# Identity and ones matmuls for three sums of a sparse-plus-polynomial attention layer (four-layer GNN, fp32)

## The chip, the cores and the metric

The kernel runs on one core of a Trainium2 chip. The metric is the device time of one execution in microseconds; three runs of the kernel before gave 3329.15, 3336.72 and 3339.13 us, and the median, 3336.72 us, is "the time before". Lower is better.

## The reference

Four graph layers over N = 2708 nodes with 128 features, all fp32, each on the ReLU of a layer norm of x and added back to x. Only layer 1 is touched by the change. With n nodes, H = 8 components and a reshape that mixes nodes and columns, it computes

```
q = (x @ Wq.T).reshape(d, n, h)          # d = 128 heads, h = 8
k = (x @ Wk.T).reshape(d, n, h)
v = (x @ Wv.T).reshape(d, n, h)
a = einsum('dnh,dmh->dnm', q, k) * d ** (-0.5)
a = softmax(a + adj + adj, axis=2)
out = einsum('dnm,dmh->dnh', a, v).reshape(n, h * d)
x = x + out @ Wo.T
```

So there are 128 heads (the index d), and each has queries, keys and values of only 8 components. adj is sparse: about four random entries in a row and the diagonal.

## The kernel before, in words

Layer 1 is not computed as 128 dense 2708 x 2708 attentions. The logits q.k are small, so exp(q.k) is written as a polynomial of degree 4. The sum over all nodes m then factors into products of monomials, and only the few neighbours of a node, where adj is not zero, are handled exactly by an added term with the weight exp(2 adj) - 1.

**The polynomial, one head at a time** (`for d in range(D)` in the block under `tc.manual_schedule()`, 128 heads; the order of every instruction there is the order in which the Python code issues it). N is cut into NT = 22 row tiles of 128 (the last has 20 rows), and these into NCH = 6 chunks of 4, 4, 3, 4, 4, 3 tiles; `parts` are the two halves of 11 tiles.
- `keys(d)` and `queries(d)` build, from the eight components, B_ALL = 9 second monomials (one and the eight components, in bk and bq) and F_ALL = 128 first monomials (fk and fq). ScalarE makes copies and squares (L717 to L719), `features` makes the products: for queries all by VectorE (L1147), for keys by GpSimd (L1150) except one of the last four products, which VectorE makes. `copies` (L1163) puts keys and queries in PSUM for VectorE.
- `with_values(d, h)` makes y, the values (8 and a one, VW = 9) times the second monomials of the key (copy by ScalarE L1181, product by GpSimd L1150).
- `moments(d, ...)` sums fk times y over the nodes on TensorE into m_ps (L1200), `weighted(d)` scales the result into mw (VectorE, L1210).
- `turn(d, c)` transposes the query monomials of a chunk on TensorE into f_ps (L1226), ScalarE copies them to fT (L1228). f_ps lies in the pool ps_t, which has a single PSUM buffer under the tag "tr".
- `evaluate(d, c)` multiplies fT by mw on TensorE into g_ps (L1238). VectorE multiplies by the query's second monomials into z (L1246), and **adds over the nine second monomials** with a reduction into o_raw (L1252).
- In a chunk the order is evaluate(d, c), turn(d, c+1), moments(d+1, ...), so a head's moments are made a head ahead; the sixth chunk has no moments.
- `prepare(g)` loads a group of GRP = 4 heads into raw and also **adds up all values** of the four heads: VectorE reduces raw over the row tiles (v_part, L806), TensorE adds over the partitions with ones (v_t, L813 and L815), VectorE copies to v_sum (L817). `sums(g)`, after the last head of a group, adds v_sum (the constant term of the polynomial) to o_raw on GpSimd (L824) and stores o_g.

**Beside it** a generator `first` is stepped 1.5 times in every chunk (PACE): `by_node` rewrites keys, values and queries by node to DRAM (n_kv, n_q, ScalarE L855, two groups to a store), `sorted_rows` loads the sorted lists of neighbours, and `from_neighbours` takes 121 blocks. A block is one neighbour slot for 128 nodes: a gather c_kv (GpSimd DMA, L915), the products of key and query for 128 heads times 8 components c_z (GpSimd, L930), **their sum over the eight components** c_c (VectorE reduction, L936), exp and weight (ScalarE, L943 and L944), weight times value c_v (VectorE, L954), and the accumulation over a node's slots on TensorE with an identity into v_ps (L971). After a tile's last slot `store` copies v_ps to c_acc (L986) and the result is scattered to more_n.

When `first` has ended, `step` runs `normalise` (load o_g and more_n, GpSimd adds them L1047, VectorE divides L1051 and L1052, store) and `project_out` (load o_cr, eight matmuls with woT, L676). woT, the transposed Wo, is made ahead of the loop by `load_wo` (L659 to L666).

Bold names the three sums that the change moves.

Of the kernel before, what the change touches and what calls it, by code (L numbers as in the profile page):

```python
# [45 lines left out]
def gnn4_kernel(  # L46
# [610 lines left out]
    def load_wo(lp, wk_pool, ps, tag):  # L657
        wo_nat = wk_pool.tile([P, HD], FP, name="wo_nat", tag=tag)
        nc.sync.dma_start(wo_nat, wo)  # L659
        wo_h = wo_nat.rearrange("p (c k) -> p k c", k=HEAD)  # L660
        woT = lp.tile([P, HEAD, C], FP, name="woT")
        for k0, kw in _cuts(HEAD, 4):
            pt = ps.tile([P, 4, C], FP, name="wo_ps", tag="tr")
            for k in range(kw):
                nc.tensor.transpose(pt[:, k], wo_h[:, k0 + k], ident)
            nc.vector.tensor_copy(woT[:, k0 : k0 + kw], pt[:, :kw])  # L666
        return woT
# [18 lines left out]
    with ExitStack() as ph:  # L686
# [3 lines left out]
        tm = ph.enter_context(tc.tile_pool(name="l1_tm", bufs=2))  # L690
        sm = ph.enter_context(tc.tile_pool(name="l1_sm", bufs=2))
        fp = ph.enter_context(tc.tile_pool(name="l1_f", bufs=2))
        ftp = ph.enter_context(tc.tile_pool(name="l1_ft", bufs=3))
# [11 lines left out]
        def features(mul, k, b, f, kp=None, other=None):  # L705


            n, T = k.shape[:2]
            kp = k if kp is None else kp
            kh = kp.rearrange("p t (h e) -> p t h e", h=2)  # L710
            ks = k.rearrange("p t (h e) -> p t h e", h=2)
            two, two_s = (a.rearrange("p t (x w) -> p t x w", w=2) for a in (kp, k))
            inn = b[:, :, 9:21].rearrange("p t (h e) -> p t h e", h=2)
            crs = b[:, :, 21:29].rearrange("p t (h e) -> p t h e", h=2)
            mul2, kp2 = (mul, kp) if other is None else other
            kh2 = kp2.rearrange("p t (h e) -> p t h e", h=2)
            nc.scalar.copy(b[:, :, 1:9], k)  # L717
            nc.scalar.copy(f[:, :, :8], k)
            nc.scalar.activation(inn[:, :, :, :4], ks, AF.Square)  # L719
            mul(  # L720
                inn[:, :, :, 4:6],
                two[:, :, :, 0].rearrange("p t (h x) -> p t h x", h=2),
                two_s[:, :, :, 1].rearrange("p t (h x) -> p t h x", h=2),
            )
            yield
            for a in range(2):
                mul(
                    crs[:, :, :, 2 * a : 2 * a + 2],
                    kh[:, :, :, 2:4],
                    ks[:, :, :, a : a + 1].to_broadcast([n, T, 2, 2]),  # L730
                )
                yield
            o = 8
            for h in range(2):
                mul(
                    f[:, :, o : o + 16].rearrange("p t (a b) -> p t a b", a=4),
                    kh[:, :, h, :, None].to_broadcast([n, T, 4, 4]),
                    inn[:, :, h, None, :4].to_broadcast([n, T, 4, 4]),
                )
                yield  # L740
                o += 16
            three = f[:, :, o : o + 8].rearrange("p t (h a b) -> p t h a b", h=2, a=2)
            for a in range(2):
                mul(
                    three[:, :, :, a],
                    kh[:, :, :, 2 - 2 * a : 4 - 2 * a],
                    inn[:, :, :, 4 + a : 5 + a].to_broadcast([n, T, 2, 2]),
                )
                yield
            o += 8  # L750
            for src, w in ((inn, 6), (crs, 4)):
                for h in range(2):
                    m, of = (mul2, kh2) if w == 6 and h else (mul, kh)
                    m(
                        f[:, :, o : o + 4 * w].rearrange("p t (a b) -> p t a b", a=w),
                        src[:, :, h, :, None].to_broadcast([n, T, w, 4]),
                        of[:, :, 1 - h, None, :].to_broadcast([n, T, w, 4]),
                    )
                    yield
                    o += 4 * w  # L760
            assert o == F_ALL
# [25 lines left out]
        def prepare(g, got):  # L787
# [6 lines left out]
            for e, at in enumerate((q_at, k_at)):  # L794
# [9 lines left out]
            v = raw[:, :, :, 2 * HEAD :]  # L804
            part = sm.tile([P, GRP, VW], FP, name="v_part")
            nc.vector.reduce_sum(  # L806
                part, v[:, :, :NF].rearrange("p i t k -> p i k t"), axis=AX.X
            )
            yield
            pt = ps_t.tile([P, BK], FP, name="v_t", tag="tr")  # L810
            to = pt[:, : GRP * VW]
            flat = part.rearrange("p i k -> p (i k)")
            nc.tensor.matmul(to, ones, flat, start=True, stop=not REM)  # L813
            if REM:
                nc.tensor.matmul(to, ones[:REM], v[:REM, :, NF], start=False, stop=True)  # L815
            vs = sm.tile([P, GRP, VW], FP, name="v_sum")
            nc.vector.tensor_copy(vs.rearrange("p i k -> p (i k)"), pt[:, : GRP * VW])  # L817
            got.append((raw, vs))
            yield

        def sums(g, ro):

            vs = got[g][1]
            nc.gpsimd.tensor_tensor(  # L824
                ro, ro, vs[:, None].to_broadcast([P, NT, GRP, VW]), ALU.add
            )
            nc.sync.dma_start(o_g[g], ro.rearrange("p t i k -> p (t i k)"))

        def by_node():
# [11 lines left out]
            for j in range(NG):  # L841
# [3 lines left out]
                if j % 2 == 0:  # L845
                    kv = lp.tile(
                        [P, NT, 2, GRP, 2, HEAD], FP, name="n_kv", tag="n_kv", bufs=2
                    )
                    qn = lp.tile([P, NT, 2, GRP, HEAD], FP, name="n_q", bufs=1)
# [8 lines left out]
                if j % 2:  # L858
                    hs = slice((j - 1) * GRP, (j + 1) * GRP)
# [31 lines left out]
        def from_neighbours():  # L891
# [34 lines left out]
            def logits(b):  # L926
                t, s0, w = todo[b]
                sz = rows[t][1]
                zs[b] = tm.tile([P, C, HEAD], FP, name="c_z", tag="tmp")
                nc.gpsimd.tensor_tensor(zs[b][:sz], kvs[b][:sz, 0, :, 0], qs[t][:sz], ALU.mult)  # L930

            def summed(b):
                t, s0, w = todo[b]
                sz = rows[t][1]
                cs[b] = c_two[:, b % 2, 0]
                nc.vector.reduce_sum(cs[b][:sz], zs.pop(b)[:sz], axis=AX.X)  # L936

            def weigh(b):
# [3 lines left out]
                c = cs[b][:sz]  # L942
                nc.scalar.activation(c, c, AF.Exp)  # L943
# [5 lines left out]
            def values(b):  # L949
# [3 lines left out]
                vs[b] = z = tm.tile([P, 2, BK // HEAD, HEAD], FP, name="c_v", tag="c_v")  # L953
# [10 lines left out]
            def added(b):  # L964
# [3 lines left out]
                if s0 == 0:  # L968
                    accs[t] = ps_v.tile([P, 2, BK], FP, name="v_ps")
                for j in range(2):  # L970
# [4 lines left out]
                        start=s0 == 0,  # L975
# [5 lines left out]
            def store():  # L981
                while done:
# [7 lines left out]
                    nc.scalar.copy(acc[:sz, :, HEAD], dens.pop(t)[:sz])  # L990
# [8 lines left out]
            if REM:  # L999
                none = tm.tile([P, C // 2 * VW], FP, name="none", tag="tmp")  # L1000
                nc.gpsimd.memset(none, 0.0)
# [7 lines left out]
            for b in range(M + 2):  # L1009
                if b + 1 < M:  # L1010
                    load(b + 1)
                yield
# [4 lines left out]
                if 0 < b <= M:  # L1017
                    weigh(b - 1)
                if 1 < b:
                    added(b - 2)  # L1020
                yield
# [3 lines left out]
                yield  # L1025
                if b < M:
                    summed(b)
# [5 lines left out]
        def normalise(g, ring):  # L1033

            if ring == "tm":
                ro = tm.tile([P, NT, GRP, VW], FP, name="r_raw", tag="tmp")
# [25 lines left out]
        woT = load_wo(lp, big, ps_t, "big")  # L1062
# [20 lines left out]
        def bank(t):  # L1083

            if not banks:
                banks.append(ps_v.tile([P, 2, BK], FP, name="v_ps"))
            return banks[0][:, t % 2, :C]

        def begin(summed):

            if not beside or beside[0][1] >= summed:
# [4 lines left out]
            for ring in ("tm", "big") if norm else ("big",):  # L1096
                if len(rings[ring]) < room[ring]:
                    beside.pop(0)
                    gen = (
                        normalise(i, ring) if norm else project_out(big, "big", bank, woT, i)  # L1100
# [57 lines left out]
        def copies(dk, dq):  # L1158

            kq = ps_q.tile([P, 2, NT, HEAD], FP, name="kq_ps")  # L1160
            for i, (what, d, at) in enumerate((("k", dk, k_at), ("q", dq, q_at))):
                if d is not None and d < D:
                    nc.scalar.copy(kq[:, i], got[d // GRP][0][:, d % GRP, :, at])  # L1163
                    copied[what, d] = kq[:, i]

        def keys(d):

            k = got[d // GRP][0][:, d % GRP, :, k_at]
# [3 lines left out]
        def with_values(d, h):  # L1172
# [3 lines left out]
            v = got[d // GRP][0][:, d % GRP, t0:t1, 2 * HEAD :]  # L1176
# [11 lines left out]
        def queries(d):  # L1188

            k = got[d // GRP][0][:, d % GRP, :, q_at]  # L1190
# [3 lines left out]
        def moments(d, h, n0, n1):  # L1194

            if d not in pms:
                pms[d] = ps_m.tile([P, BK], FP, name="m_ps")
# [32 lines left out]
        def evaluate(d, c):  # L1230
            h, t0, n = chunks[c]
            g, i = d // GRP, d % GRP
            if g not in ros:
                ros[g] = kp.tile([P, NT, GRP, VW], FP, name="o_raw")
            pg = ps_g.tile([P, 4, BK // 4], FP, name="g_ps")
            ft = fts.pop((d, c))
            for m in range(n):
# [7 lines left out]
            z = tm.tile([P, 4, VW, B_ALL], FP, name="z")  # L1245
            nc.vector.tensor_tensor(  # L1246
                z[:, :n],
# [4 lines left out]
            nc.vector.reduce_sum(  # L1252
                ros[g][:, t0 : t0 + n, i],
                z[:, :n],
                axis=AX.X,
            )

        with tc.manual_schedule():
# [20 lines left out]
            for d in range(D):  # L1279
                asked = queries(d + 1) if d + 1 < D else iter(())  # L1280
                for c in range(NCH):
# [16 lines left out]
                    elif d + 1 < D:  # L1298
                        turn(d + 1, 0)
                    if d + 1 < D and c < len(at):  # L1300
# [16 lines left out]
                g = d // GRP  # L1317
                if d % GRP == GRP - 1:
                    sums(g, ros.pop(g))
# [4 lines left out]

            nc.vector.memset(top, 0.0)
# [447 lines left out]
```

## Time and profile before

| | us |
|---|---|
| median of the three runs | 3336.72 |
| the profiled execution, its own time | 3354.19 |
| the span of that execution on the core | 3352.4 |
| busy PE (matmul) / PEld (weight load) | 2691.7 / 2273.0 |
| busy DVE / POOL / ACT | 2202.7 / 2009.3 / 1314.8 |

The profiled execution is 17.5 us longer than the median. The loop over heads runs from 563 us (its first mw) to 2830 us of the span; the text calls 563 to 970 us stage A (by_node beside the heads, 24 heads), 970 to 2373 us stage B (the neighbours' blocks, 81 heads) and 2373 to 2830 us stage C (normalise and project, 23 heads). What comes before is layer 0 and the making of q, k and v; what comes after is layers 2 and 3.

In the profile's lines, PE is TensorE's matmul, PEld its weight load, DVE is VectorE, ACT is ScalarE, POOL is GpSimd, SP the queue that issues most DMAs. Every fp32 matmul that is not a transpose stands in the trace as two records ("passes" in the text), each with a weight load of its own: L1238 issues 2816 matmuls and has 5632 records. A matmul's record lasts past the start of the next one, since they are pipelined; what a pass occupies is the distance from its start to the next start.

### The profile page before, as it was taken

To read this page: it belongs to the slowest core of one execution; us is meant where nothing else is said; L and a number is where in the kernel's file an instruction comes from. 1 tells how busy PE (TensorE), PEld (TensorE's weight loads), DVE (VectorE), ACT (ScalarE), POOL (GpSimd) and SP (SyncE) were. 2 spreads that over 40 slices of the span, in tenths; PEclk is the share of its full clock that TensorE was granted. 3 is DMA by queue.
4 is the path that set the end of the run, shared out by engine and by line. 5 is a ranking of instruction groups with operands and counts; after the bars stand their busy time and mean duration, and the time that the engine had idled before them with its cause. 6 is when DMAs were issued, how large, how long until landed. Compare 5 with 4: busy or idle time off the path is not lost. (4 is left out here: it accounts for less than half of the span.)

```text
span 3352.4 us, 50866 instructions
## 1 busy us (share of the span) xinstructions
PE 2691.7 (80%) x17781; PEld 2273.0 (68%) x17781; DVE 2202.7 (66%) x5135; ACT 1314.8 (39%) x3127; POOL 2009.3 (60%) x2263
## 2 busy tenths in 40 slices
PE   6477884888789999999999999999888897796044
PEld 4476543777788887888888788877777886443033
DVE  3868753666678888888888788887666675213222
ACT  3485462555544444444444444444322232102010
POOL 0111115555588888888988888889656663000775
PEclk6688896999999999999999999999888999895565
DMA  3452274777743333333334333343465712541322
GB/s 113 175 227 93 76 326 128 208 214 206 211 131 114 125 125 127 128 132 128 119 138 139 126 141 125 137 143 121 94 148 143 166 48 64 193 176 56 106 83 61
DMA packets 312741, 462.08 MB, mean 138 GB/s; under 512 B 159650, under 2 KB 234404, under 8 KB 289330
## 3 DMA queue, kind: packets, MB, share of 16 engines
q1 hardware_dynamic: 280870, 289.79, 28.3%
q0 software_dynamic: 31600, 168.86, 14.7%
q8 instruction: 148, 2.42, 0.3%
q14 instruction: 123, 1.01, 0.1%
HBM read 344.89 MB, written 113.67 MB: 137 GB/s over the span
## 5 line engine op out<-in xcount | busy, mean ns | idle before, releaser
L1238 PE MATMUL g_ps<-mw,fT 128*128 128x128 f32 x5632 | 817.5, 287 | 155.2 <-ACT fT L1228 115.1
L1238 PEld LDWEIGHTS g_ps<-mw,fT 128*128 128x128 f32 x5632 | 715.4, 196 | 290.6 <-ACT fT L1228 178.4
L1228 ACT COPY fT<-f_ps 128x512 f32<-128x512 f32 (+1 forms) x768 | 420.6, 548 | 1216.7 <-PE f_ps L1226 1216.6
L1200 PE MATMUL m_ps<-y,fk 128*128 128x128 f32 (+1 forms) x5632 | 768.2, 280 | 0.0
L1200 PEld LDWEIGHTS m_ps<-y,fk 128*128 128x128 f32 (+1 forms) x5632 | 699.9, 194 | 15.4
L1150 POOL TENSOR_TENSOR y<-bk,raw 128x792 f32<-128x792 f32 x256 | 415.8, 1624 | 432.1 <-ACT y L1181 420.3
L1246 DVE TENSOR_TENSOR z<-g_ps,bq 128x324 f32<-128x324 f32 (+1 forms) x768 | 355.6, 463 | 435.0 <-PE g_ps L1238 433.6
L1226 PE MATMUL f_ps<-ident,fq 128*128 128x128 f32 x2816 | 441.6, 276 | 14.4 <-DVE v_sum L817 9.3
L1252 DVE TENSOR_REDUCE o_raw<-z 128x36 f32<-128x324 f32 (+1 forms) x768 | 355.8, 463 | 26.4
L1150 POOL TENSOR_TENSOR fk<-bk,raw 128x352 f32<-128x352 f32 (+1 forms) x384 | 357.7, 955 | 0.1
L1226 PEld LDWEIGHTS f_ps<-ident,fq 128*128 128x128 f32 x2816 | 340.2, 144 | 16.2 <-DVE v_sum L817 10.6
L1150 POOL TENSOR_TENSOR fk<-raw,bk 128x352 f32<-128x352 f32 (+1 forms) x512 | 312.6, 640 | 3.1 <-ACT bk L719 2.3
L1147 DVE TENSOR_TENSOR fq<-bq,kq_ps 128x528 f32<-128x528 f32 (+1 forms) x512 | 288.2, 605 | 0.0
L930 POOL TENSOR_TENSOR c_z<-c_kv,c_q 128x1024 f32<-128x1024 f32 (+1 forms) x121 | 284.2, 2349 | 2.2 <-DMA c_kv<-kv_n,srt 1.4
L971 PE MATMUL v_ps<-c_v,ident 128*128 128x512 f32 (+1 forms) x484 | 233.3, 605 | 15.3 <-ACT c_acc L986 15.3
L1591 POOL DMA_INDIRECT g<-gate_d,srt x121 | 120.4, 995 | 110.2 <-issue 109.0
L1147 DVE TENSOR_TENSOR fq<-kq_ps,bq 128x352 f32<-128x352 f32 (+1 forms) x512 | 171.9, 378 | 0.0
L155 POOL CAST n_fl<-n_ci 128x40 f32<-128x40 int32 (+1 forms) x22 | 4.8, 218 | 251.9 <-DVE n_ci L138 251.9
L936 DVE TENSOR_REDUCE c_c<-c_z 128x128 f32<-128x1024 f32 (+1 forms) x121 | 147.5, 1219 | 3.4 <-POOL c_z L930 3.2
L954 DVE TENSOR_TENSOR c_v<-c_kv,c_c 128x1024 f32<-128x1024 f32 (+1 forms) x121 | 146.7, 1212 | 0.0
L971 PEld LDWEIGHTS v_ps<-c_v,ident 128*128 128x128 f32 (+1 forms) x484 | 82.0, 189 | 79.1 <-issue 58.8
L915 POOL DMA_INDIRECT c_kv<-kv_n,srt x121 | 117.8, 974 | 23.1 <-issue 9.6
(290 smaller groups left out, 3714.1 us busy)
## 6 DMA issues: line engine op xcount, KB each, us to landing
a_nat<-in_adj_dram SPq DMA_DIRECT2D x34, 1354.0 KB
qkv_c<-qkv SPq DMA_DIRECT2D x5, 6400.0 KB
a<-in_adj_dram SPq DMA_DIRECT2D x21, 1354.0 KB
kv_n<-n_kv SPq DMA_DIRECT2D x16, 1344.0 KB
o_g<-o_raw SPq DMA_DIRECT2D x32, 396.0 KB
q_n<-n_q SPq DMA_DIRECT2D x16, 672.0 KB
o_cr<-o_c SPq DMA_DIRECT2D x21, 512.0 KB
r_raw<-o_g SPq DMA_DIRECT2D x22, 396.0 KB
```

What stands on the lines that cost most here:

```text
L930: nc.gpsimd.tensor_tensor(zs[b][:sz], kvs[b][:sz, 0, :, 0], qs[t][:sz], ALU.mult)
L936: nc.vector.reduce_sum(cs[b][:sz], zs.pop(b)[:sz], axis=AX.X)
L954: nc.vector.tensor_tensor(z[:sz], kv[:sz, 0, :, 1].rearrange("p (j c) k -> p j c k", j=2), c.rearrange("p (j c) -> p j c", j=2)[:, :, :, None]
L971: nc.tensor.matmul(accs[t][:sz, j], ident[:sz, :sz], z[:sz, j].rearrange("p c k -> p (c k)"), start=s0 == 0, stop=s0 == ROOM[t] - 1,)
L1147: nc.vector.tensor_tensor(o, x, y, ALU.mult)
L1150: nc.gpsimd.tensor_tensor(o, x, y, ALU.mult)
L1200: nc.tensor.matmul(pms[d][:, :P], fks[d][:sz, t], ys[d, h][:sz, m * VW * B_ALL : m * VW * B_ALL + P], start=t == 0, stop=t == NT - 1,)
L1226: nc.tensor.transpose(pt[:, m], fqs[d][:, t0 + m], ident)
L1228: nc.scalar.copy(fts[d, c][:, :n], pt[:, :n])
L1238: nc.tensor.matmul(pg[:, m], ft[:, m], mws[d], start=True, stop=True,)
L1246: nc.vector.tensor_tensor(z[:, :n], pg[:, :n, : B_ALL * VW].rearrange("p t (k b) -> p t k b", k=VW), bqs[d % 2][:, t0 : t0 + n, None, :B_A ...
L1252: nc.vector.reduce_sum(ros[g][:, t0 : t0 + n, i], z[:, :n], axis=AX.X,)
```

## The change

Seven things change, all in layer 1.
1. `evaluate` no longer reduces z. z is one tile for half a head, laid out with the second monomial outermost, written by the same VectorE products. A new `add_up`, called in the sixth chunk between turn and the next head's evaluate for the second half of the last head and the first half of this one, adds the nine slices of 99 columns with identity matmuls into o_ps, which shares the one buffer of m_ps. ScalarE copies o_ps to o_raw, and after the last head of a group o_g is stored.
2. The neighbours' products c_z are written with the component outermost (a step of 512 bytes between writes), and eight identity matmuls of 128 columns add them into c_l, in the one "tr" buffer of ps_t. exp reads c_l. `summed` and `weigh` of a block now come at the start of the next block's steps.
3. `prepare` no longer adds up values and `sums` is gone. `all_values` adds the values of eight heads over all nodes from n_kv, with 22 matmuls whose stationary operand is one column of ones, into a row v_row. That row starts the accumulation of each of the 22 node tiles in v_ps, through a matmul with one row of ones as stationary operand; the denominators get N as a bias of the copy to c_acc, and the padding rows are set to one instead of zero.
4. `load_wo` moves from ahead of the loop to the first call of `begin`, at the start of stage C. woT takes the place of n_q.
5. For keys, both products of the six-wide inner monomials (each 128 x 528 elements) are made by VectorE; before, it was one of the two.
6. A pool tz with three buffers holds z, c_z, c_v, none and r_raw; c_z and c_v share a tag.
7. fT has two buffers instead of three.

```diff
-        ftp = ph.enter_context(tc.tile_pool(name="l1_ft", bufs=3))
+        tz = ph.enter_context(tc.tile_pool(name="l1_tz", bufs=3))
+        ftp = ph.enter_context(tc.tile_pool(name="l1_ft", bufs=2))
...
-                    m, of = (mul2, kh2) if w == 6 and h else (mul, kh)
+                    m, of = (mul2, kh2) if w == 6 else (mul, kh)
...
-            part = sm.tile([P, GRP, VW], FP, name="v_part")
-            nc.vector.reduce_sum(
-                part, v[:, :, :NF].rearrange("p i t k -> p i k t"), axis=AX.X
-            )
...
-            nc.tensor.matmul(to, ones, flat, start=True, stop=not REM)
-            if REM:
-                nc.tensor.matmul(to, ones[:REM], v[:REM, :, NF], start=False, stop=True)
-            vs = sm.tile([P, GRP, VW], FP, name="v_sum")
-            nc.vector.tensor_copy(vs.rearrange("p i k -> p (i k)"), pt[:, : GRP * VW])
...
-            nc.gpsimd.tensor_tensor(
-                ro, ro, vs[:, None].to_broadcast([P, NT, GRP, VW]), ALU.add
-            )
-            nc.sync.dma_start(o_g[g], ro.rearrange("p t i k -> p (t i k)"))
+        def all_values(kv, j):
+
             pt = ps_t.tile([P, BK], FP, name="v_t", tag="tr")
+            w = 2 * GRP * HEAD
+            to = pt[0:1, :w].rearrange("p (j i k) -> p j i k", j=2, k=HEAD)
+            for t, (_, sz) in enumerate(rows):
+                nc.tensor.matmul(
+                    to, ones[:sz, 0:1], kv[:sz, t, :, :, 1], start=t == 0, stop=t == NT - 1
+                )
+            nc.scalar.copy(vrow[:, (j // 2) * w : (j // 2 + 1) * w], pt[0:1, :w])
...
                 if j % 2:
+                    all_values(kv, j)
...
-                nc.gpsimd.tensor_tensor(zs[b][:sz], kvs[b][:sz, 0, :, 0], qs[t][:sz], ALU.mult)
+                zs[b] = tz.tile([P, HEAD, C], FP, name="c_z", tag="tmp")
+                nc.gpsimd.tensor_tensor(
+                    zs[b][:sz].rearrange("p k c -> p c k"),
+                    kvs[b][:sz, 0, :, 0],
+                    qs[t][:sz],
+                    ALU.mult,
+                )
...
-                nc.vector.reduce_sum(cs[b][:sz], zs.pop(b)[:sz], axis=AX.X)
+                z = zs.pop(b)
+                cs[b] = ps_t.tile([P, BK], FP, name="c_l", tag="tr")[:, :C]
+                for k in range(HEAD):
+                    nc.tensor.matmul(
+                        cs[b][:sz], ident[:sz, :sz], z[:sz, k],
+                        start=k == 0, stop=k == HEAD - 1,
+                    )
...
-                nc.scalar.activation(c, c, AF.Exp)
+                nc.scalar.activation(c, cs[b][:sz], AF.Exp)
...
                 if s0 == 0:
                     accs[t] = ps_v.tile([P, 2, BK], FP, name="v_ps")
+                    for j in range(2):
+                        nc.tensor.matmul(
+                            accs[t][:sz, j],
+                            ones[0:1, :sz],
+                            vrow[:, j * BK : (j + 1) * BK],
+                            start=True,
+                            stop=False,
+                        )
...
             for b in range(M + 2):
                 if b + 1 < M:
                     load(b + 1)
+                if 0 < b <= M:
+                    summed(b - 1)
+                    weigh(b - 1)
                 yield
...
-        woT = load_wo(lp, big, ps_t, "big")
...
             if not banks:
+                banks.append(load_wo(lp, big, ps_t, "big", "n_q"))
...
-            z = tm.tile([P, 4, VW, B_ALL], FP, name="z")
+            if t0 == parts[h][0]:
+                zt[d, h] = tz.tile([P, B_ALL, TM, VW], FP, name="z")
+            m0 = t0 - parts[h][0]
             nc.vector.tensor_tensor(
-                z[:, :n],
+                zt[d, h][:, :, m0 : m0 + n].rearrange("p b t k -> p t k b"),
...
-            nc.vector.reduce_sum(
-                ros[g][:, t0 : t0 + n, i],
-                z[:, :n],
-                axis=AX.X,
-            )
...
+        def add_up(which):
+
+            which = [(d, h) for d, h in which if 0 <= d < D]
+            ps = ps_m.tile([P, BK], FP, name="o_ps", tag="m_ps")
+            at = 0
+            for d, h in which:
+                T = parts[h][1] - parts[h][0]
+                z = zt.pop((d, h))
+                for b in range(B_ALL):
+                    nc.tensor.matmul(
+                        ps[:, at : at + T * VW],
+                        ident,
+                        z[:, b, :T],
+                        start=b == 0,
+                        stop=b == B_ALL - 1,
+                    )
+                at += T * VW
...
+                nc.scalar.copy(
+                    ros[g][:, t0:t1, i],
+                    ps[:, at : at + T * VW].rearrange("p (t k) -> p t k", k=VW),
+                )
+                at += T * VW
+                if h and i == GRP - 1:
+                    ro = ros.pop(g)
+                    nc.sync.dma_start(o_g[g], ro.rearrange("p t i k -> p (t i k)"))
...
+                    if c == NCH - 1:
+                        add_up([(d - 1, 1), (d, 0)])
...
+            add_up([(D - 1, 1)])
```

## The prediction

> **What bounds the kernel now.** I first read the busy time by stage, then the groups the change touches, then TensorE's timeline, since a busy share alone doesn't tell whether an engine sets the pace. By stage (columns: window, its length, then PE, PEld, DVE, ACT and POOL busy, then granted clock, DMA share, GB/s):
>
> ```profile
> 563.00:970.00 407.00, 338.48 (x2664) 318.09 (x2664) 263.82 (x636) 221.05 (x497) 238.99 (x321) 0.94 0.70 192
> 970.00:2373.00 1403.00, 1313.53 (x9463) 1131.45 (x9464) 1156.64 (x2488) 609.28 (x1641) 1221.70 (x1275) 0.99 0.37 128
> 2373.00:2830.00 457.00, 385.05 (x2804) 364.48 (x2804) 300.55 (x673) 140.76 (x364) 272.33 (x290) 0.94 0.47 111
> ```
>
> These are stages A, B and C. In B, PE is busy 94%, POOL 87%, DVE 82%. The groups that go:
>
> ```profile
> L1252 DVE TENSOR_REDUCE o_raw<-z 128x36 f32<-128x324 f32 (+1 forms) x768 | 355.8, 463 | 26.4
> L936 DVE TENSOR_REDUCE c_c<-c_z 128x128 f32<-128x1024 f32 (+1 forms) x121 | 147.5, 1219 | 3.4 <-POOL c_z L930 3.2
> L824 POOL TENSOR_TENSOR o_raw<-o_raw,v_sum 128x792 f32<-128x792 f32 x32 | 59.8, 1870 | 25.1 <-DVE top L1325 25.0
> ```
>
> Whether DVE or POOL can bound is told by TensorE's timeline over a head late in stage C, where nothing runs beside it:
>
> ```profile
> 2767.39 0.94 PE L1238 MATMUL g_ps<-mw,fT 128*128 128x128 f32 x6
> 2768.16 0.60 PE L1226 MATMUL f_ps<-ident,fq 128*128 128x128 f32 x4
> 2769.49 1.16 PE L1238 MATMUL g_ps<-mw,fT 128*128 128x128 f32 x8 [0.73 <-ACT fT L1228]
> 2770.48 0.60 PE L1226 MATMUL f_ps<-ident,fq 128*128 128x128 f32 x4
> 2770.92 1.06 PE L1200 MATMUL m_ps<-y,fk 128*128 128x128 f32 x8
> 2772.35 1.16 PE L1238 MATMUL g_ps<-mw,fT 128*128 128x128 f32 x8 [0.37 <-ACT fT L1228]
> ...
> 2774.56 0.83 PE L1238 MATMUL g_ps<-mw,fT 128*128 128x128 f32 x6
> 2775.23 0.60 PE L1226 MATMUL f_ps<-ident,fq 128*128 128x128 f32 x4
> 2775.67 0.83 PE L1200 MATMUL m_ps<-y,fk 128*128 128x128 f32 x6
> ...
> 2780.50 1.47 PE L1200 MATMUL m_ps<-y,fk 128*128 128x128 f32 x10
> 2781.90 2.41 PE L676 MATMUL v_ps<-woT,o_cr 128*128 128x128 f32 x9
> ```
>
> Starts follow one another without a hole: 6 g passes take 2774.56 to 2775.23, or 111.5 ns each, 4 transposes 0.44 us. The head runs from 2767.39 to 2781.90, 14.5 us. Waits are two: the f passes end near 2768.60 and g starts at 2769.49 (0.89 us, for fT), and m ends near 2771.81 and g starts at 2772.35 (0.54 us). So 13.1 us is issue and 1.4 us waiting. A block adds four passes of 512 columns:
>
> ```profile
> 1510.84 1.88 PE L971 MATMUL v_ps<-c_v,ident 128*128 128x512 f32 x4
> 1512.56 0.83 PE L1238 MATMUL g_ps<-mw,fT 128*128 128x128 f32 x6
> ```
>
> 1.72 us, 0.43 each. Stage B then has 81 x 14.5 + 121 x 1.72 = 1383 us against 1403 measured: a head that runs beside full DVE and POOL costs what the quiet head costs plus its extra passes. **TensorE bounds**, with small waits; DVE and POOL run in its shadow. Its real idle time: B 1403 - 81 x 13.1 - 208 = 134; A 407 - 24 x 13.1 = 93; C 457 - 23 x 13.1 - 69 (288 L676 passes at about 0.24) = 87. Together about 314 us.
>
> **What the Trainium skill says.** "Perfetto Trace Analysis", Identifying the Most-Contended Engine, warns that matmul busy time misleads because pipelined matmuls overlap, and asks for weight-load busy. Here that is 81% in B, so it too leaves TensorE the tightest. "TensorE: Matmul & The Clock Gate", LDWEIGHTS, gives a weight load columns / 1.2 ns: 107 ns for 128 columns, whatever streams. The 109 to 112 ns spacings agree; no long run here has fewer than 128 columns. The same page, Back-to-back issue gap, gives about 216 ns for 512 columns; this trace has 0.43 us for each of two fp32 passes, and the measurement decides. "SBUF — State Buffer", Door 1 (its note on cachelines), says that accesses leaving a 16-byte line pay a penalty; z and c_z are now written with steps of 396 and 512 bytes, which no run here shows.
>
> **The change part by part**, against the profiled 3354.19 us.
>
> *Sum of z.* 128 heads x 2 halves x 9 matmuls = 2304, two passes each, as L971 with the same identity shows: 4608 passes of 99 columns. Not shown; bounds are the column rate (0.43 us / 512 x 99 = 0.083 us, 382 us in all) and the 128-column pass (0.1115, 514). If the identity's 128-column load sets it, as the page implies, the narrow stream gains nothing: I take 0.108, **+498 us**. All of it is on the path, since it is PE's own queue.
>
> *Sum of logits.* 121 x 8 x 2 = 1936 passes of 128 columns at 0.1115: **+216**. Bounds 0.109 and 0.1115 come from the f and g rows, +211 to +216.
>
> *All values.* 16 stores x 22 x 2 = 704 passes of 64 columns with one stationary column. Below, the column rate, 0.054 (+38); above, a load not overlapped, 0.107 + 0.054 = 0.16 (+113); I take 0.08, **+56**. Their start in v_ps: 22 x 2 x 2 = 88 passes of 512 columns with one row, 0.43 to 0.43 + 0.107 each (+38 to +47), **+42**. In exchange v_t goes: in the timeline at 1201.61 its four passes hold PE 0.64 us, and the lines view puts 23.1 us of PE waits on v_part: 32 x 0.64 + 23 = **-44**.
>
> *Waits at the head's edge.* add_up stands where PE waited 0.89 us for fT: that goes. But ScalarE now waits for add_up before two o_raw copies (0.37 each by L1181's row, in order) and then makes one y copy, two kq_ps copies and six feature copies, some 2.5 us, before fT of the second chunk. Counting from add_up's end, fT lands at about 3.9 us, and PE, with g, f and m in 2.2, waits 1.7 instead of 0.54. Net +0.3 x 128 = **+38**. Bounds: both waits filled by block passes, -1.4 x 128 = -180; 1.2 us more a head, +192. Behind ScalarE's wait stand y, hence POOL's y product, already waiting 420 us in sum, and features needed a head later.
>
> *Waits that lessen.* PE waited 22 us for DVE mw, behind reductions: **-20**. In A, ScalarE waited 31.7 us for the store of n_q, and in C PE 31.0 us for o_cr; slower heads give these transfers time: **-42** of 93 + 87 idle.
>
> *Hidden at nothing.* DVE loses 355.8 + 147.5 + 51.8 + 6 and gets 128 x 0.70 = 90 from POOL, which loses 128 x 1.16 + 60. Per head of B, DVE goes from 14.3 to 10.0 us, POOL from 15.1 to 13.4, against some 24 of PE. Strided writes at double price add 2.8 and 3.5: still hidden; without cover, 356 and 284 us in all. ScalarE's 256 o_raw copies, about 95 us, fit in its 43%. The o_g store goes out a head later but normalise takes only groups two back. fT's third buffer: only two are ever live. add_up sharing m_ps must follow weighted, which DVE does 1.1 us of PE work earlier; the next moments wait for o_raw copies 0.9 us after add_up, with g and f before them in 1.3. c_l in f_ps's one buffer waits for the fT copy, behind m or add_up, and exp (0.32) is hidden behind the next g (0.9): 0, bounds 0 to +0.5 x 121 = 60.
>
> *load_wo moved.* Its DMA passes SP's queue ahead of the first r_raw loads, and eight transposes stand in PE's order behind it: 3.6 us from issue to transposes before, plus two DVE copies, **+5** (0 to +12). Ahead of the loop POOL's list scatter ends at 536 and sets the start; **-3** (-15 to +5). At the end, sums' 1.9 us goes: **-2**.
>
> Sum: 498 + 216 + 56 + 42 - 44 + 38 - 20 - 42 + 5 - 3 - 2 = +744; 3354 + 744 = 4098 profiled, or, less the 17.5 us by which that execution exceeds the median, **4081**, rounded to 4080.
>
> **The rivals.** *Cheaper passes* (0.17): the loads hide and z goes at the column rate (-116), all_values too (-18), and about half the edge waits are filled (-90): 3856. For it: weights never change in add_up. Against: each record in L971 has its own load. *New waits* (0.13): ScalarE's order costs 1.2 us more a head (+154) and c_l's buffer 0.5 a block (+60): 4294. For it: 178 us of g loads already wait for fT. Against: add_up covers one of two edges. *Faster* (0.05, with 0.01 for no change): POOL and DVE pace B, PE only follows. Keeping POOL's 87% share at 13.4 us gives 15.4 a head instead of 17.3, 81 x 1.9 = 154: 3183. It decides if 7336 added passes cost less than PE's idle time and v_t's issue, 314 + 20, or 46 ns each. For it: POOL's 87%. Against: the additive fit of B, and no pass above under 109 ns. That the sums aren't moved is excluded, as the new loops issue them unconditionally.
>
> **How the numbers follow.** Forecast 0.65 at 4080. The range of 3820 to 4250 leaves out about 0.05 of the cheaper case, 0.08 of new waits and the 0.05. About 0.3% is what a measurement of this kernel can tell from no change: faster 0.04, same 0.01, slower 0.95.
>
> **What would show it.** Right: heads of B near 24 us; o_ps starts 0.108 us apart and c_l 0.11; PE near 95% in B with DVE and POOL far below; the wait of g for fT gone in the first chunk and longer in the second. Wrong: o_ps spacing near 0.083 or below, a second 0.5 us or more of PE idle before c_l, or stage B shorter with PE less busy.

## The result, and the profile after

The changed kernel takes 4011.81 us (median of four runs, 4008.3 to 4015.08), the kernel before 3334.96 us beside it. The ratio is 1.2031 with a 95% interval of 1.2008 to 1.2054: 20% slower. 4080 us was forecast, 3820 to 4250 the range.

The table by stage of the changed kernel (same columns as before). Stages hold the same heads and blocks as before, A the first 24 heads, B the next 81, C the last 23, and are cut at the first mw of a stage, as before.

```profile
560.00:1049.00 489.00, 449.81 (x4146) 429.35 (x4144) 234.76 (x505) 233.40 (x554) 199.96 (x290) 1.00 0.58 158
1049.00:2996.00 1947.00, 1875.91 (x14335) 1674.91 (x14335) 925.34 (x1922) 652.19 (x1806) 1099.58 (x1175) 0.99 0.28 93
2996.00:3498.00 502.00, 464.14 (x3623) 450.30 (x3624) 266.08 (x544) 149.54 (x410) 235.59 (x263) 0.99 0.44 104
```

A grew by 82 us, B by 544, C by 45: 671 in all. In B, PE went from 94 to 96% busy, DVE fell from 82 to 48% and POOL from 87 to 56%. VectorE and GpSimd were relieved, and the kernel got slower by what TensorE was given. B's heads went from 17.3 to 1947 / 81 = 24.0 us. The granted clock, the column after POOL, rose from 0.94 to 1.00 in A and from 0.94 to 0.99 in C.

The groups that came (from the groups view; the last one stayed, but now writes with a step):

```profile
L1277 PE MATMUL o_ps<-z,ident 128*128 128x99 f32 x4608 | 534.8, 275 | 1.1 <-DVE mw L1224 0.6 <-ACT o_raw L1292 0.5
L936 PE MATMUL c_l<-c_z,ident 128*128 128x128 f32 (+1 forms) x1936 | 247.0, 281 | 56.0 <-POOL bk L1164 47.3 <-ACT fT L1242 6.1 <-POOL c_z L923 2.7
L816 PE MATMUL v_t<-n_kv,ones 128*1 128x64 f32 x704 | 43.3, 219 | 0.0
L975 PE MATMUL v_ps<-v_row,ones 1*128 1x512 f32 (+1 forms) x88 | 45.9, 642 | 13.7 <-ACT c_acc L998 13.7
L1259 DVE TENSOR_TENSOR z<-g_ps,bq 128x324 f32<-128x324 f32 (+1 forms) x768 | 538.8, 702 | 1304.1 <-PE g_ps L1249 1302.4
```

DVE's idle time before z is now 1304 us, ended by PE's g_ps: it waits for TensorE. In the kernel before it was 435 us. TensorE's timeline over a quiet head late in stage C:

```profile
3404.68 0.94 PE L1249 MATMUL g_ps<-mw,fT 128*128 128x128 f32 x6
3405.45 0.60 PE L1240 MATMUL f_ps<-ident,fq 128*128 128x128 f32 x4
3405.89 4.16 PE L1277 MATMUL o_ps<-z,ident 128*128 128x99 f32 x36
3409.89 1.08 PE L1249 MATMUL g_ps<-mw,fT 128*128 128x128 f32 x8
3410.80 0.60 PE L1240 MATMUL f_ps<-ident,fq 128*128 128x128 f32 x4
3411.24 1.06 PE L1214 MATMUL m_ps<-y,fk 128*128 128x128 f32 x8
3413.38 1.16 PE L1249 MATMUL g_ps<-mw,fT 128*128 128x128 f32 x8 [1.08 <-ACT fT L1242]
...
3422.99 0.94 PE L1249 MATMUL g_ps<-mw,fT 128*128 128x128 f32 x6
```

The head runs from 3404.68 to 3422.99, 18.3 us against 14.5. The 36 passes of o_ps take 3405.89 to 3409.89, 4.0 us or 0.111 each, and stand where PE waited 0.89 us for fT. The second wait has grown: m ends near 3412.13, g starts at 3413.38, 1.25 us instead of 0.54. ScalarE's timeline across that edge shows why:

```profile
3406.14 0.59 ACT L1242 COPY fT<-f_ps 128x512 f32<-128x512 f32 x1 [2.13 <-PE f_ps L1240]
3410.09 0.39 ACT L1292 COPY o_raw<-o_ps 128x99 f32<-128x99 f32 x2 [3.35 <-PE o_ps L1277]
3410.36 0.38 ACT L1195 COPY y<-raw 128x99 f32<-128x99 f32 x1
3410.54 0.76 ACT L1177 COPY kq_ps<-raw 128x176 f32<-128x176 f32 x2
...
3412.77 0.56 ACT L1242 COPY fT<-f_ps 128x512 f32<-128x512 f32 x1
```

ScalarE stands 3.35 us behind add_up, then makes o_raw, y, kq_ps and the feature copies left out here, and only then fT. Where a block's logits fall on this edge, the wait stands before c_l, which needs the buffer that fT's copy frees:

```profile
1271.72 2.02 PE L936 MATMUL c_l<-c_z,ident 128*128 128x128 f32 x16 [1.18 <-POOL bk L1164]
```

The additive sum of the prediction holds here too: 81 heads at 18.3 us, 121 blocks at 1.72 + 16 x 0.1115 us and the 42 us that start v_ps make 1948 us, against 1947 measured for B.

### The profile page after: what moved, and what is told of

It is laid out like the page before. It is cut to its first block, busy times and chain, and to the rows that moved or that the text cites. A ratio compares the mean times of both kernels' runs of the same rounds, so it can differ in the third digit from the quotient of the medians.

```text
span 4006.5 us, 64678 instructions
## 1 busy us (share of the span) xinstructions
PE 3455.6 (86%) x24989; PEld 3023.8 (75%) x24989; DVE 1906.1 (48%) x4310; ACT 1378.4 (34%) x3399; POOL 1807.6 (45%) x2103
## 5 line engine op out<-in xcount | busy, mean ns | idle before, releaser
L1259 DVE TENSOR_TENSOR z<-g_ps,bq 128x324 f32<-128x324 f32 (+1 forms) x768 | 538.8, 702 | 1304.1 <-PE g_ps L1249 1302.4
L1249 PE MATMUL g_ps<-mw,fT 128*128 128x128 f32 x5632 | 789.4, 282 | 72.5 <-ACT fT L1242 55.6
L1277 PE MATMUL o_ps<-z,ident 128*128 128x99 f32 x4608 | 534.8, 275 | 1.1 <-DVE mw L1224 0.6
L1277 PEld LDWEIGHTS o_ps<-z,ident 128*128 128x128 f32 x4608 | 526.7, 193 | 1.7 <-DVE mw L1224 1.0
L936 PE MATMUL c_l<-c_z,ident 128*128 128x128 f32 (+1 forms) x1936 | 247.0, 281 | 56.0 <-POOL bk L1164 47.3
L923 POOL TENSOR_TENSOR c_z<-c_kv,c_q 128x1024 f32<-128x1024 f32 (+1 forms) x121 | 285.3, 2358 | 3.7 <-DMA c_kv<-kv_n,srt 2.9
L936 PEld LDWEIGHTS c_l<-c_z,ident 128*128 128x128 f32 (+1 forms) x1936 | 225.6, 191 | 74.3 <-POOL bk L1164 53.7
L983 PE MATMUL v_ps<-c_v,ident 128*128 128x512 f32 (+1 forms) x484 | 244.2, 629 | 0.0
L1164 POOL TENSOR_TENSOR fk<-bk,raw 128x352 f32<-128x352 f32 x256 | 215.4, 855 | 0.1
L1161 DVE TENSOR_TENSOR fk<-bk,kq_ps 128x528 f32<-128x528 f32 x256 | 168.6, 700 | 97.4 <-POOL bk L1164 90.9
L1292 ACT COPY o_raw<-o_ps 128x99 f32<-128x99 f32 x256 | 50.3, 251 | 436.7 <-PE o_ps L1277 436.7
```

The source lines that it names most:

```text
L923: nc.gpsimd.tensor_tensor(zs[b][:sz].rearrange("p k c -> p c k"), kvs[b][:sz, 0, :, 0], qs[t][:sz], ALU.mult,)
L936: nc.tensor.matmul(cs[b][:sz], ident[:sz, :sz], z[:sz, k], start=k == 0, stop=k == HEAD - 1,)
L983: nc.tensor.matmul(accs[t][:sz, j], ident[:sz, :sz], z[:sz, j].rearrange("p c k -> p (c k)"), start=False, stop=s0 == ROOM[t] - 1,)
L1161: nc.vector.tensor_tensor(o, x, y, ALU.mult)
L1164: nc.gpsimd.tensor_tensor(o, x, y, ALU.mult)
L1249: nc.tensor.matmul(pg[:, m], ft[:, m], mws[d], start=True, stop=True,)
```

## The experiments

The theory: TensorE's in-order queue is the bound before and after; each added pass is paid in full, about 791 us by the starts in the trace (4608 x 0.1115 + 1936 x 0.1115 + 39 for all_values + 22 x 1.91 for the starts of v_ps, less 20 for v_t of before), and only waits can give something back. The rivals: waits and shared buffers make up much of the loss; or VectorE and GpSimd have a say in the pace. Every ratio below is to the kernel before on the same chip. It gave 3335.03 us beside the sum of z undone, the first sum of logits undone, the wider passes and the transposes ahead of g; 3354.16 us beside the second sum of logits undone, the later copies, all values alone and z read with a step; 3352.41 us beside the last two. So kernels are compared by ratio, with 1.2031 for the change, and a difference of ratios is turned into us at 3335 us.

**The sum of z undone.**

```diff
 in the changed kernel
-            zt[d, h][:, :, m0 : m0 + n] <- products;  add_up(...)
+            z = tz.tile([P, 4, VW, B_ALL], FP, name="z")
+            nc.vector.reduce_sum(ros[g][:, t0 : t0 + n, i], z[:, :n], axis=AX.X)
```

> The changed kernel with its first part alone undone: VectorE again reduces z chunk by chunk, nothing else differs. Theory (TensorE's in-order queue is the bound, and every added pass is paid in full): 4608 passes at 0.1115 us, 514 us, go, and the head's edge gets its 0.89 us wait for fT back but loses about 0.7 us of the later wait, so 3.8 us a head come off, 486 us: about 3526 us, 3490 to 3560. Rival (ScalarE's blocked queue and shared buffers were the larger part of the loss): clearly below 3450. Rival (VectorE or GpSimd pace the heads): above 3900.

Measured: 3564.91 us, just above the expected range; ratio 1.0688 (1.0665 to 1.0711). So 0.134 of the 0.203 is the z sum, 447 us. By stage:

```profile
558.00:968.00 410.00, 364.94 (x3336) 339.26 (x3335) 268.93 (x648) 224.95 (x509) 199.66 (x291) 1.00 0.69 188
968.00:2605.00 1637.00, 1564.61 (x11418) 1350.44 (x11418) 1059.20 (x2409) 621.28 (x1644) 1098.09 (x1175) 0.98 0.33 111
2605.00:3063.00 458.00, 385.43 (x2790) 365.76 (x2789) 306.34 (x682) 140.55 (x364) 236.79 (x263) 0.93 0.48 111
```

B lost 310 us, 3.8 a head as expected. C lost only 44, or 1.9 a head: once heads are short again, TensorE waits 37.1 us in C for o_cr, against 4.4 in the changed kernel, and the granted clock in C is 0.93 again. That is most of the 39 us by which the expectation missed. Both rivals' figures are out.

**The sum of logits undone, twice.** First alone, in the new order of a block's steps; then with the steps of before.

```diff
 in the changed kernel
-                for k in range(HEAD):
-                    nc.tensor.matmul(cs[b][:sz], ident[:sz, :sz], z[:sz, k], ...)
+                nc.vector.reduce_sum(cs[b][:sz], zs.pop(b)[:sz], axis=AX.X)
 and, in the second kernel only
-                if 0 < b <= M:
-                    summed(b - 1)
-                    weigh(b - 1)
...
+                if 0 < b <= M:
+                    weigh(b - 1)
...
+                if b < M:
+                    summed(b)
```

> The changed kernel with its second part alone undone: c_z is laid out as before and VectorE reduces it. Theory: 1936 passes at 0.1115 us, 216 us, and most of the 56 us in which TensorE stood before c_l go: about 3750 us, 3720 to 3800. If GpSimd's or VectorE's load mattered beside TensorE, the VectorE reduction of 1.22 us a block would be felt and the time would stay above 3850.

> The changed kernel with the second part undone, and the steps of a block back in the order of before: the VectorE reduction in a block's last step, exp three steps later. With the reduction but the new order the time was 3879 us, not the 3750 expected, and ScalarE stood 179 us in stage B before exp, waiting for the reduction that is issued in the same step, with fT and c_acc behind it. If that order is the cause, most of the 92 us of idle time it added goes: 3780 us, 3745 to 3800. If VectorE's or GpSimd's load is the cause, it stays near 3879.

Measured: 3878.78 us, 1.1637 (1.1617 to 1.1656) for the first, a miss by 129 us that lands on the rival's figure, above 3850; 3815.58 us, 1.1371 (1.1352 to 1.139) for the second, which is 3792 us at the first chip's pace and inside the range expected. The first trace's waits in stage B (us in total, times, longest) begin with a wait of exp for VectorE; in the second trace that wait is gone, and the other two are as shown below it:

```profile
ACT c_c L936 <- DVE c_c L929: 178.8, 81, 4.6
PE g_ps L1239 <- ACT fT L1232: 66.8, 66, 1.1
PE v_ps L965 <- ACT c_acc L988: 46.7, 21, 3.3
...
PE g_ps L1240 <- ACT fT L1233: 48.1, 52, 1.9
PE v_ps L965 <- ACT c_acc L988: 14.3, 21, 1.6
```

exp is issued in the same step as the reduction it reads, ScalarE stands up to 4.6 us behind VectorE's queue, and PE pays for fT and c_acc behind it. These two PE waits are 51 us less in the second kernel, and the granted clock in B is 0.98 there instead of 0.96, worth at most 0.02 x 1800 = 36 us by estimate; together that is about the 89 us between the two ratios. With the order of before, the ratio falls 0.066 below the change's: 220 us, against 216 us of passes. So the first kernel had tested a step order together with the sum; VectorE's and GpSimd's work is the same in both, so their load isn't what held it up.

**Wider passes.** One z tile for two halves, 9 matmuls of 198 columns instead of 18 of 99 (two small tiles move to another pool to make room).

```diff
 in the changed kernel
+                zt[d + h] = tz.tile([P, B_ALL, 2 * TM, VW], FP, name="z", bufs=2)
...
-                        z[:, b, :T],
+                    z[:, b, a0 : a0 + len(which) * TM],
```

> The changed kernel with both halves' z in one tile, so that nine matmuls of 198 columns do the work of eighteen of 99. The sums are the same. If a pass of 99 columns is set by the load of its 128-column identity, a pass of 198 columns costs the column rate, 0.43 us / 512 x 198 = 0.166 us, and a head's 18 passes 2.99 us instead of 4.01: 1.02 x 128 = 130 us less, about 3880 us, 3850 to 3905. If the time of a pass goes with its columns (0.1115 us for 99), nothing is gained: 4012 us within 15.

Measured: 3891.6 us, 1.1675 (1.1653 to 1.1698), 120 us less than the change, in the range of the first case. Its timeline:

```profile
3312.55 3.19 PE L1276 MATMUL o_ps<-z,ident 128*128 128x198 f32 x18
3315.58 1.05 PE L1249 MATMUL g_ps<-mw,fT 128*128 128x128 f32 x8
```

18 passes in 3.03 us, 0.168 each: twice the columns for 1.5 times the time. At 99 columns a pass had a floor, and the columns were not it. That fits a floor from loading 128 identity columns; the load wasn't varied by itself.

**ScalarE's copies later.** The o_ps copies are issued in the next head's first chunk, behind its feature copies.

```diff
 in the changed kernel
+                    if c == 0 and d:
+                        copy_out()      # the nc.scalar.copy loop of add_up
                     if c + 1 < NCH:
                         turn(d, c + 1)
```

> The changed kernel, with the two ScalarE copies of o_ps issued later: in the next head's first chunk, after the y, kq_ps and feature copies, just ahead of that chunk's transposes, instead of right behind add_up's matmuls. No work is added or removed. If TensorE's remaining wait at the head's edge (1.25 us before the second chunk's g, or before c_l in its place) comes from ScalarE standing behind add_up before its copies, the copies now run during add_up and the wait goes: 1.0 to 1.25 us a head, 130 to 160 us less, 3850 to 3885 us. If the wait has another cause (the one buffer of f_ps, GpSimd's products), 4012 within 20.

Measured: 3913.82 us, 1.1676 (1.1656 to 1.1695): 0.0355 below the change, 118 us, a little short of the 130 to 160 expected. The same edge now:

```profile
3314.49 4.16 PE L1277 MATMUL o_ps<-z,ident 128*128 128x99 f32 x36
3318.49 1.08 PE L1249 MATMUL g_ps<-mw,fT 128*128 128x128 f32 x8
3319.40 0.60 PE L1240 MATMUL f_ps<-ident,fq 128*128 128x128 f32 x4
3319.84 1.06 PE L1214 MATMUL m_ps<-y,fk 128*128 128x128 f32 x8
3320.73 1.10 PE L1249 MATMUL g_ps<-mw,fT 128*128 128x128 f32 x8
```

g follows m without a hole. The waits before c_l at this edge, put down to bk in the changed kernel (47.3 us in stage B), are gone as well. So the remaining edge wait comes from ScalarE's order; neither the single buffer nor GpSimd makes it. Why the gain is 0.9 and not 1.25 us a head, no run shows.

**All values alone**, on the kernel before.

```diff
 in the kernel before
-            nc.vector.reduce_sum(part, ...);  two matmuls;  nc.vector.tensor_copy(vs, ...)
+                    all_values(kv, j)
-            nc.gpsimd.tensor_tensor(ro, ro, vs[:, None]..., ALU.add)
```

> The kernel before with the third part alone: all_values from n_kv with a column of ones, v_row starting v_ps, no v_part, v_t of before or sums (fT with two buffers for the space). By the trace of the changed kernel, all_values holds TensorE 39 us and the start of v_ps 40 us; 15 to 20 us of v_t issue and 23 us of waits on v_part go: 36 to 41 us more, 3375 us, 3350 to 3395. If taking 52 us from VectorE and 60 from GpSimd counts, the time is at or below 3335.

Measured: 3384.02 us, 1.0083 (1.0065 to 1.0101), 22 to 34 us more. Freeing both engines gave no net gain. In sum the passes were paid, a little less than counted, but not stage by stage: A, which holds the 39 us of all_values, grew by 5 us while its granted clock rose from 0.94 to 1.00, and B grew by 37 us, with its clock down from 0.99 to 0.97, where the passes that came less those of v_t make about 30.

**z written without a step, read with one.**

```diff
 in the changed kernel
-                zt[d, h] = tz.tile([P, B_ALL, TM, VW], FP, name="z")
+                zt[d, h] = tz.tile([P, TM, VW, B_ALL], FP, name="z")
-                        z[:, b, :T],
+                        z[:, :T, :, b],
```

> The changed kernel with z laid out as in the kernel before (the second monomial innermost): VectorE writes z without a step, and TensorE reads its slices with a step of 36 bytes instead. VectorE's product of z should fall from 0.70 us back to 0.46 us. Since VectorE is hidden, the time says what the stepped read costs TensorE: 4012 us within 15 if nothing, up to about 4500 if a pass of 99 columns doubles.

Measured: 4340.11 us, 1.2943 (1.2921 to 1.2964), 0.091 or 304 us above the change. Two lines of the groups, then one of its timeline and its follower:

```profile
L1277 PE MATMUL o_ps<-z,ident 128*128 128x99 f32 x4608 | 849.5, 358 | 0.5 <-ACT o_raw L1292 0.5
L1259 DVE TENSOR_TENSOR z<-g_ps,bq 128x324 f32<-128x324 f32 (+1 forms) x768 | 357.9, 466 | 1685.0 <-PE g_ps L1249 1677.6 <-PE c_l L936 6.6
```

```profile
1313.36 6.63 PE L1277 MATMUL o_ps<-z,ident 128*128 128x99 f32 x36
1319.81 1.90 PE L983 MATMUL v_ps<-c_v,ident 128*128 128x512 f32 x4
```

VectorE's z falls from 702 to 466 ns, 181 us in all, and buys nothing. TensorE's 36 passes take 6.45 us instead of 4.0, 0.179 each; 4608 x 0.068 = 313 us, against a loss of 304. The change's layout, which gives the step to the hidden engine, was the right one of the two.

**Transposes ahead of g**, on the kernel before, moves no sum and aims at TensorE's waits alone.

```diff
 in the kernel before
+                    if c + 1 < NCH:
+                        turn(d, c + 1)
+                    elif d + 1 < D:
+                        turn(d + 1, 0)
                     evaluate(d, c)
...
-                    if c + 1 < NCH:
-                        turn(d, c + 1)
-                    elif d + 1 < D:
-                        turn(d + 1, 0)
```

> The kernel before with one move: the transposes of the next chunk are issued ahead of the g matmuls of this one, instead of after them; no sum is moved. If TensorE bounds and its waits are those for fT at the head's edge (0.89 and 0.54 us a head), about 0.9 us of them go: 115 us less, about 3220 us, 3180 to 3270. If GpSimd (87% busy in stage B) or VectorE (82%) paces the heads, nothing is gained or z comes later: 3325 to 3360 us.

Measured: 3268.92 us, 0.980 (0.9784 to 0.9816): **faster than both kernels**, 66 us below the one before, just inside the expected range, with 57% of the gain at its middle. VectorE's and GpSimd's work is unchanged, so they didn't set the pace. TensorE's waits in stage B, first in the kernel before, then in this one, show that fT's went and v_part's grew:

```profile
PE g_ps L1238 <- ACT fT L1228: 35.8, 85, 0.7
PE g_ps L1238 <- DVE mw L1210: 21.9, 17, 1.6
PE v_t L813 <- DVE v_part L806: 13.6, 15, 1.3
...
PE v_t L813 <- DVE v_part L806: 35.3, 20, 1.8
PE g_ps L1238 <- DVE mw L1210: 17.0, 21, 3.8
PE f_ps L1226 <- ACT fT L1228: 6.9, 12, 0.7
```

**And v_t two steps later**, to take that v_part wait away too.

```diff
 in the kernel with the transposes first
             nc.vector.reduce_sum(part, ...)
             yield
+            yield
+            yield
```

> The kernel before with the transposes ahead of the g matmuls, and with two more steps between VectorE's reduction v_part and the matmuls v_t that wait for it. In the trace of the first alone TensorE waits 35 us in stage B for v_part, at the head of its queue. If TensorE's waits are what is left to win, those go: about 1% less than the first alone, a ratio of 0.970 to the kernel before (0.965 to 0.975; the first alone had 0.980). If VectorE and GpSimd, 86 and 91% busy by then in stage B, hold the heads, the ratio stays at 0.980.

Measured: 3314.63 us, 0.988 (0.9864 to 0.9897): worse than without, and outside both figures. The wait did go, and another came:

```profile
PE f_ps L1228 <- DVE v_sum L819: 59.2, 20, 3.0
```

v_t sits in the one "tr" buffer that the transposes need, until VectorE copies v_sum; at its new place that copy starts 2.7 us after v_t's end (median), not 1.6, behind more of VectorE's queue.

**Key products alone**, on the kernel before.

```diff
 in the kernel before
-                    m, of = (mul2, kh2) if w == 6 and h else (mul, kh)
+                    m, of = (mul2, kh2) if w == 6 else (mul, kh)
```

> The kernel before with the fifth part alone: both six-wide inner products of the keys by VectorE, 90 us more for it and 148 us less for GpSimd. If both are hidden behind TensorE the time doesn't move: a ratio of 0.997 to 1.004. If VectorE's load is felt, up to 1.027; if GpSimd's was, down to 0.97.

Measured: 3380.95 us, 1.0084 (1.0068 to 1.0101): 28 us slower, so not hidden. VectorE's busy time rose by 79 us, not 90, and about a third of that is felt; in stage B, PE's waits for mw, v_part and z are 26.8, 19.1 and 9.6 us, against 21.9, 13.6 and none in the kernel before. VectorE isn't the bound, but TensorE meets its queue at a few points. B grew by 16 us and C by 12; what C lost isn't traced to one wait.

## Why the prediction was right, step by step

**The bound and the passes: right.** The parts account for the whole: z 0.134, logits 0.066 and all values 0.008 add to 0.208, with the key products 0.216, against 0.203 for all together. The forecast put 792 us of issue on TensorE net of v_t's issue (498 + 216 + 56 + 42 - 20); the trace has 791. That it is so close is luck in part, since two terms were off in opposite directions: z at 0.108 us a pass was 0.1115, 514 us, and all_values at 0.08 was 0.056, 39 us, close to its column rate. One argument for the bound was read wrongly: weight-load busy is 81% in B, below POOL's 87% and DVE's 82%, so by that measure TensorE was not the tightest. What carries the bound is the sum of the quiet head and its extra passes.

**The waits: too little was given back.** The loop grew 671 us, so 120 of the 314 us of idle time were absorbed, where the steps held -23 for v_part, +38 at the edges, -20 for mw and -42 for transfers, -47 in all. By stage, passes less growth leave about 44 us absorbed in A, 26 in B and 51 in C. No single step holds the miss.
- *Waits at the head's edge*, "+0.3 x 128 = +38": the mechanism is there, as the later copies show, and the wait was taken too long. fT landed about 3.5 us after add_up's end, not 3.9: the o_raw copies are 251 ns, not the 0.37 taken from L1181's row, and they overlap. So PE waits 1.25 us in a quiet head, not 1.7, which with 1.43 before is 0.18 less instead of 0.3 more. Over a stage it is mixed: with those before c_l, PE's waits for fT in B rose from 35.8 to 54.5 us, and in C they stayed (18.3 and 17.6).
- Transfers gave about what was counted: PE's wait for o_cr in C fell from 31.0 to 4.4 us; in A, ScalarE's wait for the store of n_q fell from 31.7 to 0.4 us and PE's wait for fT behind it from 61.0 to 36.9. Waits of the transposes for v_sum, 9 us in A and C, went too and were in no step.
- The granted clock was in no step either. In the kernel before, A and C have it at 0.94. After a hole of 3.82 us at the start of stage B, eight g passes take 1.84 us, 0.23 each instead of 0.111, and the granted clock of 969 to 977 us is 0.57:

```profile
970.77 2.05 PE L1238 MATMUL g_ps<-mw,fT 128*128 128x128 f32 x8 [3.82 <-ACT kq_ps L1163]
972.61 1.06 PE L1226 MATMUL f_ps<-ident,fq 128*128 128x128 f32 x4
```

The prediction's idle time, a stage less 13.1 us a head, holds such slow passes. With the clock at 1.00 and 0.99, A and C gain at most 0.06 x 407 = 24 and 0.05 x 457 = 23 us of the 120, an estimate from the stage tables; no run varies the clock alone.

**Outside the loop.** The two profiles also differ by 17 us there, mostly after the loop. The kernels of all runs, which share that code, took 499 to 529 us for it, so no cause in the change is claimed.

**Hidden at nothing: half right.** In the changed kernel it holds: z's product costs 0.70 us for 0.46 and c_z's 2358 ns for 2349, and in the stepped-read kernel 181 us less of VectorE's work brought no gain that shows beside TensorE's 313. For the kernel before, "DVE and POOL run in its shadow" was too strong: key products alone cost 28 us. In the change no cost of theirs shows, as the other three parts add to 0.208 alone. The likely cover, not tested by itself, is that VectorE is busy 297 us less in all: 561 us of reductions and copies are gone, some 260 us of stepped writes and key products have come.

**The rivals.** *Faster* is out: TensorE's busy share rose and the others' fell. *Cheaper passes* is out: the spacing is 0.111, not 0.083. *New waits* had the place right and the size wrong: the sign it gave, PE idle for 0.5 us or more before c_l, did appear, 40 times in B, but it is the edge wait of the heads whose block falls there, and it goes with the later copies.

## What to carry to other kernels

Before moving work to another engine, take one quiet iteration from that engine's timeline, split it into issue and waiting, and check that the busy iterations cost just the quiet one plus their extra passes; if they do, that engine is the bound, however busy the others look, and added passes are paid in full. Gains then lie in its waits: moving the transposes ahead was worth 2%, where taking 297 us of busy time from VectorE came with a loss of 20%, since TensorE was given 791. Put an instruction and its reader on an in-order engine some steps apart, and look for the wait that takes the place of the one you remove.

## What the runs showed of the hardware that was not expected

- An fp32 pass of 99 columns under a 128-column identity starts every 0.1115 us, one of 128 columns as well, one of 198 every 0.168, one of 512 every 0.43; 64 columns under a single stationary column every 0.056.
- A moving operand read with a step of 36 bytes takes 0.179 us for those 99 columns.
- VectorE's write with a step of 396 bytes costs half as much again (466 to 702 ns), GpSimd's with 512 bytes nothing (2349 to 2358 ns). The Trainium skill's "SBUF — State Buffer", Door 1, names a penalty for leaving a line; here a stepped write cost more on one of the two engines; that the line is the cause isn't shown.
